# A two-layer attention block on one core: first scores between the query units, another order at the opening and the group norm, an earlier check of sums

## The chip, the cores and the metric

The kernel runs on one core of one Trainium2 chip. The metric is device time in microseconds (us) of one launch, measured over several executions. Names of engines as in the profile: PE is TensorE's matmul, PEld its weight load, DVE VectorE, ACT ScalarE, POOL GpSimd, SP SyncE.

## The reference

Input x has the shape (8, 512, 32, 32) in float32: 8 batches, 512 channels, 1024 tokens. There are two layers in a row:

```python
# layer 0: layer norm over channels, 8 heads of 64, residual
xn = layer_norm(x_flat, gamma, beta)
q = xn @ Wq.T + bq; k = xn @ Wk.T + bk; v = xn @ Wv.T + bv
attn = softmax(q k^T / 8)          # per head
out = (attn v) @ Wo.T + bo + residual
# layer 1: group norm (32 groups), one head of 512, residual
h = group_norm(x, gamma, beta)
q = wq h + bq; k = wk h + bk; v = wv h + bv
attn = softmax(q^T k / sqrt(512))
return x + wp (attn v) + bp
```

## The kernel before

All products of 512 x 512 blocks and larger are done as seven half-size products instead of eight (a class `Product` with seven steps; each step is four matmul records of 128x512 or eight of 128x256). The sums of blocks that this needs are made once per weight by GpSimd, and per batch by VectorE (the differences T1 to T4 of an activation, `T_h` in the profile for the layer norm's result). In an opening, two weight products are formed: a = wk^T wq for layer 1's scores, and m = wp wv. Names that recur: lns and lnq are VectorE's sums of x and of its centred squares, over which PE forms mean and var for the layer norm; psbm, psbo and psu are groups of 32 one-column matmuls that make three small vectors; pm and pv are PE's sums of the group norm's statistics mv and gdev; "half clock" is a granted clock of 0.5 for PE's array. PE's order is fixed by hand; the order of the other engines is the scheduler's.

```python
def sums_of_blocks(engine, w, view=lambda t: t):      # GpSimd, for the weights
    engine.tensor_add(w["S1"], w["21"], w["22"])
    engine.tensor_sub(w["S2"], w["S1"], w["11"])
    engine.tensor_sub(w["S3"], w["11"], w["21"])
    engine.tensor_sub(w["S4"], w["12"], w["S2"])
...
def add_operands(b, names):                            # VectorE, T1 to T4
    for n in names:
        ...
        nc.vector.tensor_sub(wide(b[n]), wide(b[l]), wide(b[r]))
...
nq = natural(wq, "q1")                 # 32 transposes on PE, 2 copies on ACT
ln = LayerNorm(0, x_next)
for k in range(NH):
    ln.sums(k)                         # lns, on VectorE
ln.mean()                              # 2 x 2 matmul records
for k in range(NH):
    ln.centre(k); ln.squares(k)        # lnq, on VectorE
nk = natural(wk, "k1")
columns(bm, ...)                       # psbm: 32 one-column matmul records
product(wa, nq, nk, "a", 0)
ln.deviation()                         # var
...
product(wa, nq, nk, "a", 1)
... sums_of_blocks(nc.gpsimd, wo), and of w_v, w_q, wa, wm on GpSimd too ...
nv = natural(wv, "v1")
columns(bo, ...)                       # psbo
product(wm, nv, wp, "m", 0); product(wm, nv, wp, "m", 1)
kt = all_of(project("k0", wk_now, bias_of("bk0"), hb))
columns(ua, ...)                       # psu: 32 one-column matmul records
vts = all_of(project_v("v0", wv_now, hb))
qt = all_of(project("q0", wq_now, bias_of("bq0"), hb))
```

## Time and profile before

| | before |
|---|---|
| median of 3 executions when the prediction was made | 3069.1 us (3067.01 to 3069.84) |
| span of the profiled execution | 3066.4 us |
| PE busy | 3008.8 us, 98% |
| first key projection starts | 73.37 us |
| first value projection starts | 101.11 us |
| a batch from its query projection to the next key projection | 148.4 us |
| last matmul to end of span | 8.69 us |

PE is the bound: there are 57.6 us in which it does not work. A change of order can win only parts of this, what stands in the opening at a low clock, and matmuls that it takes away. How the lines of the page, the waits, the chain and the opening are read is told in the prediction. Here are lines in PE's timeline (start, duration, instructions; in brackets the idle time and who ended it). The group norm's boundary of the second batch:

```profile
685.50 1.88 PE L330 MATMUL x_k<-x,w_k 128*128 128x512 f32 x4
687.88 0.39 PE L489 MATMUL pm<-mv,grp 128*128 128x4 f32 x2 [0.51 <-DVE mv L485]
```

The last batch's output projection:

```profile
2880.01 2.46 PE L330 MATMUL x_out<-o,w_o 128*128 128x512 f32 x4 [2.64 <-DVE u(0, 0)_out L599]
2882.26 3.15 PE L330 MATMUL z_out<-o,w_o 128*128 128x512 f32 x4
2885.25 1.88 PE L330 MATMUL x_out<-T_o,w_o 128*128 128x512 f32 x4
```

Here the reader is to see the 2.64 us wait, and behind it 2.46 and 3.15 us for groups that take 1.88 elsewhere: a stretch at half clock.

### The profile page before, as it was taken

The numbers are of one execution on the slowest core, as the hardware profiler recorded it, in microseconds if no ns is written. First come the engines' busy times: TensorE is split into PE (matmuls) and PEld (weight loads), VectorE is DVE, ScalarE is ACT, GpSimd is POOL, SyncE is SP. The second block draws the span as 40 slices with busy tenths as digits, with TensorE's granted clock in tenths as the row PEclk, the third lists the DMA queues.
The fourth block names the chain that finished last, engine by engine and source line by source line (L and its number), as shares of the span: only waits on it lengthen the run. The fifth ranks groups of instructions, "written<-read, shape, count | busy, mean of one in ns | idle before, by whom it ended". The sixth has DMA issues, their size and how long they took to land.

```text
span 3066.4 us, 26320 instructions
## 1 busy us (share of the span) xinstructions
PE 3008.8 (98%) x10098; PEld 1391.7 (45%) x10098; DVE 1807.9 (59%) x2442; ACT 1016.2 (33%) x1319; POOL 48.5 (2%) x57
## 2 busy tenths in 40 slices
PE   7999999999999999999999999999999999999898
PEld 4533455334553345433564345533455334553344
DVE  4288453874448744586446855378553785537744
ACT  3264212623136230362204612155121642215230
POOL 5000000000000000000000000000000000000000
PEclk8999999999999999999999999999999999999999
DMA  7201322012220213203032030310412004220101
GB/s 261 106 15 35 120 86 97 1 56 99 96 87 1 96 59 106 76 4 127 24 107 76 4 127 29 129 49 8 147 55 103 25 11 144 72 79 11 49 4 53
DMA packets 70616, 217.04 MB, mean 71 GB/s; under 512 B 12817, under 2 KB 16913, under 8 KB 64337
## 3 DMA queue, kind: packets, MB, share of 16 engines
q1 hardware_dynamic: 62032, 204.23, 18.9%
q0 software_dynamic: 2112, 11.01, 0.9%
q8 instruction: 81, 1.33, 0.2%
q10 hardware_dynamic: 6336, 0.03, 0.1%
q14 instruction: 55, 0.44, 0.0%
HBM read 156.00 MB, written 59.24 MB: 70 GB/s over the span
## 4 chain that ended last, share of the span: by engine, by line
PE 88%; DVE 7%; ACT 3%; issue 1%; DMA 1%; ACTq 0%; SPq 0%; DVEq 0%
PE acc L562 13%; PE s L546 13%; PE x_s L347 5%; PE x_o L355 5%; PE y_s L347 4%; PE y_o L355 4%; PE z_s L347 4%; PE z_o L355 4%; PE x_qa L330 3%; PE x_vm L339 3%; PE x_v L339 3%; PE x_q L330 3%; PE x_k L330 2%; PE y_qa L330 2%; PE y_q L330 2%; PE x_out L330 2%
## 5 line engine op out<-in xcount | busy, mean ns | idle before, releaser
L549 ACT ACTIVATE p<-s 128x1024 f32<-128x1024 f32 x512 | 483.7, 1032 | 202.3 <-PE s L546 201.7
L555 DVE TENSOR_TENSOR sum<-sum,p 128x1024 f32<-128x1024 f32 x384 | 470.0, 1224 | 53.3 <-ACT p L549 19.9
L562 PE MATMUL acc<-p,v 128*64 128x512 f32 x2048 | 465.9, 598 | 0.0
L546 PE MATMUL s<-q,k_again 64*128 64x512 f32 x1792 | 416.2, 603 | 10.0 <-ACT p L549 10.0
L546 PEld LDWEIGHTS s<-q,k_again 64*128 64x128 f32 x1792 | 163.1, 186 | 260.9 <-issue 188.3
L562 PEld LDWEIGHTS acc<-p,v 128*64 128x64 f32 x2048 | 136.2, 136 | 315.0 <-issue 296.0
L638 ACT ACTIVATE p<-p 128x512 f32<-128x512 f32 x128 | 80.6, 630 | 141.1 <-DVE p L278 141.1
L347 PE MATMUL x_s<-S_qa,T_gn 128*128 128x512 f32 x256 | 120.9, 594 | 0.0
L355 PE MATMUL x_o<-T_p,S_vm 128*128 128x512 f32 x256 | 115.1, 592 | 0.0
L553 DVE TENSOR_TENSOR sum<-p,p 128x1024 f32<-128x1024 f32 x64 | 78.2, 1222 | 58.2 <-ACT p L549 58.2
L278 DVE TENSOR_TENSOR p<-u(1, 1)_s,y_s 128x512 f32<-128x512 f32 x32 | 22.0, 687 | 123.9 <-ACT u(1, 1)_s L360 123.9
L565 ACT COPY o<-acc 128x512 f32<-128x512 f32 x64 | 37.6, 587 | 154.8 <-PE acc L562 154.8
L278 DVE TENSOR_TENSOR y<-u(1, 1)_o,y_o 128x512 f32<-128x512 f32 x16 | 11.0, 688 | 130.8 <-ACT u(1, 1)_o L360 130.8
L377 ACT ACTIVATE u(0, 0)_k<-x_k,vecs 128x512 f32<-128x512 f32 x16 | 11.0, 687 | 224.4 <-PE x_k L330 224.4
L347 PEld LDWEIGHTS x_s<-S_qa,T_gn 128*128 128x128 f32 x256 | 48.0, 190 | 63.0 <-issue 61.1
L355 PEld LDWEIGHTS x_o<-T_p,S_vm 128*128 128x128 f32 x256 | 48.6, 190 | 61.2 <-issue 61.2
L330 PE MATMUL x_out<-T_o,w_o 128*128 128x512 f32 x128 | 60.9, 598 | 2.9 <-DVE u(0, 1)_out L599 2.9
L546 PE MATMUL s<-q,k 64*128 64x512 f32 x256 | 59.5, 603 | 1.7 <-ACT p L549 1.7
L330 PE MATMUL x_qa<-T_gn,w_a 128*128 128x512 f32 x128 | 60.8, 597 | 0.0
L339 PE MATMUL x_vm<-w_m,T_gn 128*128 128x256 f32 x256 | 60.5, 379 | 0.0
L347 PE MATMUL y_s<-S_qa,gn 128*128 128x512 f32 x128 | 60.2, 592 | 0.0
L347 PE MATMUL z_s<-qa,T_gn 128*128 128x512 f32 x128 | 60.2, 592 | 0.0
(328 smaller groups left out, 4457.2 us busy)
## 6 DMA issues: line engine op xcount, KB each, us to landing
x<-in_x_dram SPq DMA_DIRECT2D x32, 512.0 KB, 9.3
xr<-in_x_dram SPq DMA_DIRECT2D x64, 256.0 KB, 3.8
x_away<-x SPq DMA_DIRECT2D x32, 512.0 KB, 3.0
x1r<-x_away SPq DMA_DIRECT2D x64, 256.0 KB, 3.8
out_dram<-y SPq DMA_DIRECT2D x64, 256.0 KB, 2.2
w_o<-saved_o SPq DMA_DIRECT2D x8, 1792.0 KB, 7.0
w_a<-saved_a SPq DMA_DIRECT2D x8, 1792.0 KB, 7.3
w_m<-saved_m SPq DMA_DIRECT2D x8, 1792.0 KB, 8.4
```

Of the source, the lines that this page charges most:

```text
L278: nc.vector.tensor_add(self.dest(i, k), u, ps)
L330: nc.tensor.matmul(dst, a[:, k, ts(r, P)], b[:, k, :], start=(opens and k == 0), stop=(k == 1), skip_group_check=True)
L339: nc.tensor.matmul(dst[:, ts(m, CB)], b[:, k, ts(2 * r + m, P)], a[:, k, :], start=(opens and m == 0 and k == 0), stop=(k == 1), skip_grou ...
L347: nc.tensor.matmul(dst, b[:, k, ts(r, P)], a[:, k, :], start=(opens and k == 0), stop=(k == 1), skip_group_check=True)
L355: nc.tensor.matmul(dst, a[:, m, ts(r, P)], b[m // 2][:, m % 2, :], start=(opens and m == 0), stop=(m == NM // 2 - 1), skip_group_check=True)
L546: nc.tensor.matmul(s[:, ts(i, HB)], self.k[m // 4][r, ts(m % 4, P)], self.q[r, :], start=True, stop=True)
L549: nc.scalar.activation(p, s, AF.Exp, scale=1.0 / float(D) ** 0.5)
L553: nc.vector.tensor_add(self.sum, self.p[0], p)
L555: nc.vector.tensor_add(self.sum, self.sum, p)
L562: nc.tensor.matmul(self.acc[i * D : (i + 1) * D, :], value_of(self.vt, m, self.c * P + i * D, D), self.p[m][:, ts(i, HB)], start=(m == 0), ...
L565: nc.scalar.copy(self.o, self.acc)
L638: nc.scalar.activation(dest(i, k), dest(i, k), AF.Exp, scale=float(C) ** -0.5)
```

## The change

Its intent: PE gets work while x and the vectors arrive, loses 32 small matmuls, starts attention's exponentials earlier, and meets fewer waits at the group norm, at the last output projection and at the end. Cut to its core:

```diff
-    wq = load_chunks("q1")
+    wq, wk = (load_chunks(n) for n in ("q1", "k1"))
+    bq1_row = half_tile("bq1_row")
+    nc.sync.dma_start(out=bq1_row, in_=...)
     x_next = load_x(0)
-    wk, wv, wp = (load_chunks(n) for n in ("k1", "v1", "p1"))
+    wv, wp = (load_chunks(n) for n in ("v1", "p1"))
 ...
         nq = natural(wq, "q1")
+        nk = natural(wk, "k1")
         ln = LayerNorm(0, x_next)
         ... sums ...
+        product(wa, nq, nk, "a", 0)
         ln.mean()
         ... centre, squares ...
-        nk = natural(wk, "k1")
+        nv = natural(wv, "v1")
+        product(wa, nq, nk, "a", 1)
         columns(bm, ...)
-        product(wa, nq, nk, "a", 0)
         ln.deviation()
         ...
-        product(wa, nq, nk, "a", 1)
-        nv = natural(wv, "v1")
-        columns(bo, ...)
         product(wm, nv, wp, "m", 0)
+        columns(bo, ...)
         product(wm, nv, wp, "m", 1)
+        for c in range(NC):
+            nc.vector.scalar_tensor_tensor(t, wk[c], 1.0, bq1_row, ..., accum_out=ua[:, c : c + 1])
         kt = all_of(project("k0", ...))
-        columns(ua, ...)
 ...
+            first = Pair(b, 0, 0, qt, kt, vts, ot)
+            first.scores(range(3))
+            q_units[1].rest()
 ...
-            groups[0][0].scores(groups[0][1])
+            first.scores(range(3, NM // 2))
 ...
-                    k_units[1].step((1, 2, 3, 1)[n])
+                    k_units[1].step((2, 1, 3, 1)[n])
 ...
-            a_units[0].step(1)
+            a_units[0].step(2)
             meanwhile(3)
-            a_units[0].step(1)
 ...
-                           banks_of(f"out_{b}", r, shared), after)
+                           banks_of(f"out_{b}", r, shared, own="x"), after)
 ...
+            if not more:
+                all_checks()
             o_units, value_sums = whole.values(vm)
```

The two query units also get PSUM tiles of their own (`apart`), and the check that stood behind the last batch became the function `all_checks`.

More of the change, by code (lines that the diff above doesn't have):

```diff
@@ L142, in load_chunks @@
         return chunks
-    wq = load_chunks("q1")
+    wq, wk = (load_chunks(n) for n in ("q1", "k1"))
+    bq1_row = half_tile("bq1_row")
+    nc.sync.dma_start(out=bq1_row, in_=vecs["bq1"].rearrange("(a c) -> a c", a=1).to_broadcast((P, C)))
     x_next = load_x(0)
-    wk, wv, wp = (load_chunks(n) for n in ("k1", "v1", "p1"))
+    wv, wp = (load_chunks(n) for n in ("v1", "p1"))
     ident = const.tile([P, P], F32, tag="ident", name="ident")
@@ L259, in columns @@
                 nc.tensor.matmul(ps[:, o : o + 1], lhs(c, o), rhs(c), start=(c == 0), stop=(c == NC - 1))
-        if plus is None:
-            nc.vector.tensor_copy(dst, ps[:, :NC])
-        else:
-            nc.vector.tensor_add(dst, ps[:, :NC], vt[:, VECS.index(plus), :])
+        nc.vector.tensor_add(dst, ps[:, :NC], vt[:, VECS.index(plus), :])
     class Product:
@@ L312, in rest, with banks_of @@
             self.step(len(STEPS) - self.done)
-    def banks_of(tag, r, shared):
+    def banks_of(tag, r, shared, own=""):
         def banks(to):
@@ L318, in banks @@
                 return bank(f"y_{tag}_{r}")
-            if shared is None:
+            if shared is None or to in own:
                 return wide_psum(f"{to}_{tag}_{r}")[:, :HB]
@@ L709, in values, with all_checks @@
             return [unit(r) for r in range(2)], lambda: sums_of_blocks(nc.vector, w, wide)
+    def all_checks():
+        one = small.tile([P, 1], F32, tag="one", name="one")
+        nc.vector.tensor_reduce(one, checks[:, : n_checks[0]], mybir.AxisListType.X, ALU.add)
+        ps = bank("ps_check")
+        nc.tensor.matmul(ps[:, :1], ones, one, start=True, stop=True)
+        ok = small.tile([P, 1], F32, tag="ok", name="ok")
+        nc.vector.tensor_scalar(ok, ps[:, :1], SUM_LIMIT, None, ALU.is_le)
+        nc.vector.tensor_scalar(flag, ok[:1, :], -1.0, 1.0, ALU.mult, ALU.add)
     def bias_of(n):
@@ L724, in fast_path @@
             ln.sums(k)
+        wa = big_slots("a")
+        product(wa, nq, nk, "a", 0)
         ln.mean()
@@ L728, in fast_path @@
             ln.squares(k)
-        nk = natural(wk, "k1")
+        nv = natural(wv, "v1")
+        product(wa, nq, nk, "a", 1)
         columns(bm, lambda c, oc: wp[c][:, ts(oc, P)], lambda c: vec("bv1", c), "bm", "bp1")
-        wa = big_slots("a")
-        product(wa, nq, nk, "a", 0)
         ln.deviation()
@@ L736, in fast_path @@
         hb = operands(ln.result())
+        add_operands(hb, ("T1", "T2", "T3", "T4"))
         wk_now = w_first["k"](nc.gpsimd)
-        add_operands(hb, ("T1", "T2", "T3", "T4"))
-        product(wa, nq, nk, "a", 1)
         wv_now = w_first["v"](nc.gpsimd)
@@ L742, in fast_path @@
         save_w("o", wo)
-        nv = natural(wv, "v1")
+        wm = big_slots("m")
+        product(wm, nv, wp, "m", 0)
         columns(bo, lambda c, oc: wo[f"{oc // 2 + 1}{c // 2 + 1}"][:, c % 2, ts(oc % 2, P)],
                 lambda c: vec("bv0", c), "bo", "bo0")
-        wm = big_slots("m")
-        product(wm, nv, wp, "m", 0)
         product(wm, nv, wp, "m", 1)
@@ L753, in fast_path @@
         save_w("m", wm)
+        for c in range(NC):
+            t = half_tile(f"uat_{c}")
+            nc.vector.scalar_tensor_tensor(t, wk[c], 1.0, bq1_row, ALU.mult, ALU.mult, accum_out=ua[:, c : c + 1])
         kt = all_of(project("k0", wk_now, bias_of("bk0"), hb))
-        columns(ua, lambda oc, c: nk[oc][:, ts(c, P)], lambda oc: vec("bq1", oc), "u", None)
         vts = all_of(project_v("v0", wv_now, hb))
-        qt = all_of(project("q0", wq_now, bias_of("bq0"), hb))
+        q_units, qt = project("q0", wq_now, bias_of("bq0"), hb, True)
+        q_units[0].rest()
         for b in range(B):
@@ L761, in fast_path @@
             ot = {"tag": f"o_{b}"}
-            pairs = [Pair(b, hf, c, qt, kt, vts, ot) for hf in range(NH) for c in range(NC)]
+            first = Pair(b, 0, 0, qt, kt, vts, ot)
+            first.scores(range(3))
+            q_units[1].rest()
+            pairs = [first] + [Pair(b, hf, c, qt, kt, vts, ot) for hf in range(NH) for c in range(NC) if hf + c > 0]
             groups = [(p, range(g * NM // 2, (g + 1) * NM // 2)) for p in pairs for g in range(2)]
             x_next = load_x(b + 1) if more else None
-            groups[0][0].scores(groups[0][1])
+            first.scores(range(3, NM // 2))
             for i, (p, ms) in enumerate(groups):
@@ L856, in fast_path @@
                 vts = all_of(project_v(f"v{b + 1}", wv_next, hb))
-                qt = all_of(project(f"q{b + 1}", wq_next, bias_of("bq0"), hb))
-        one = small.tile([P, 1], F32, tag="one", name="one")
-        nc.vector.tensor_reduce(one, checks[:, : n_checks[0]], mybir.AxisListType.X, ALU.add)
-        ps = bank("ps_check")
-        nc.tensor.matmul(ps[:, :1], ones, one, start=True, stop=True)
-        ok = small.tile([P, 1], F32, tag="ok", name="ok")
-        nc.vector.tensor_scalar(ok, ps[:, :1], SUM_LIMIT, None, ALU.is_le)
-        nc.vector.tensor_scalar(flag, ok[:1, :], -1.0, 1.0, ALU.mult, ALU.add)
+                q_units, qt = project(f"q{b + 1}", wq_next, bias_of("bq0"), hb, True)
+                q_units[0].rest()
 @with_exitstack
```

## The prediction

> **What bounds the kernel now.** I read the page first, then the list of waits of TensorE (PE), then the chain that ended last and the timeline at the four places that the change touches. The page says that PE is the bound and hardly ever stops:
>
> ```profile
> PE 3008.8 (98%) x10098; PEld 1391.7 (45%) x10098; DVE 1807.9 (59%) x2442; ACT 1016.2 (33%) x1319; POOL 48.5 (2%) x57
> ```
>
> So all that can be won without less matmul work is 3066.4 - 3008.8 = 57.6 us, plus stretches at a low clock. The list of PE's waits tells where the idle time is (columns: total, times, longest):
>
> ```profile
> PE s L546 <- ACT p L549: 11.7, 14, 1.3
> PE mean L430 <- DVE lns L438: 7.8, 2, 4.4
> PE pst_q L238 <- DMA w_q<-in_L_conv_wq_dram: 5.8, 2, 5.1
> PE pm L489 <- DVE mv L485: 5.8, 8, 2.2
> PE y_k L330 <- DVE k L278: 5.5, 7, 0.8
> PE psw_m L249 <- ACT nat_v L241: 2.9, 1, 2.9
> PE x_out L330 <- DVE u(0, 1)_out L599: 2.9, 7, 0.4
> PE x_out L330 <- DVE u(0, 0)_out L599: 2.6, 1, 2.6
> ```
>
> Three of these belong to the opening (mean, pst_q, psw_m), pm to the group norm, the last one to the eighth batch. The first line is a trap: it looks like the scores at the start of a batch, but in the timeline its 14 cases are 1.30 and 0.37 us (7 times each), beside the LayerNorm's var in the middle of a batch, where ScalarE loads two tables. At the start of a batch the chain shows PE working without a break (columns: start, us, what; it continues with the next batch's groups alike):
>
> ```profile
> 147.96 1.77 PE y_q L330 x4
> 149.72 7.07 PE s L546 x32
> 156.79 3.58 PE acc L562 x16
> 160.38 3.63 PE s L546 x16
> ```
>
> The opening, on PE alone (timeline: start, us, then the group, idle time before it in brackets):
>
> ```profile
> 14.07 2.07 PE L430 MATMUL mean<-lns,ones_c 128*128 128x512 f32 x2 [4.36 <-DVE lns L438]
> 19.59 2.08 PE L430 MATMUL mean<-lns,ones_c 128*128 128x512 f32 x2 [3.45 <-DVE lns L438]
> ...
> 29.74 9.56 PE L249 MATMUL psw_a<-nat_k,nat_q 128*128 128x512 f32 x16
> ...
> 40.85 7.03 PE L249 MATMUL psw_a<-nat_k,nat_q 128*128 128x512 f32 x16
> ...
> 57.15 16.38 PE L249 MATMUL psw_m<-w_p,nat_v 128*128 128x512 f32 x32 [2.93 <-ACT nat_v L241]
> ```
>
> The same 16 matmuls take 9.56 us the first time and 7.03 the second; the stretch table gives a mean granted clock of 0.66 for 25 to 35 us and 0.53 for 51 to 62 us, and 1.00 between and after. The key projection starts at 73.37 us.
>
> **What the Trainium skill says.** "TensorE: Matmul & The Clock Gate", section "What's actually happening": the array runs at half clock by default, and after an idle window of some 3.4 us, and at full clock after a busy one; the window runs freely. The trace agrees: half clock follows the one-column matmuls (psbm, psbo) and the idle stretches, and ends some 5 us into the dense work after them. The same page, "LDWEIGHTS (loading the stationary operand)", says that a weight load costs by its columns, P / 1.2 ns, so a one-column matmul costs a full load of 128: 107 ns. The trace: the 32 matmuls of psu take 3.47 us of the chain, 0.108 each. "ScalarE: Activation LUTs", section "What ACT_TABLE_LOAD costs": about 1283 ns a load; the trace has 1.28. "Runtime: NRT & Kernel Launch", section "Instruction fetch mechanics": a taken branch out of the fetched pages waits for its target. The trace ends with such a branch on the flag: last vector work done at 3059.8, span over at 3066.4.
>
> **Part 1, the opening.** The order of instructions becomes: transposes of w_q and w_k, product a (half 0), mean, transposes of w_v, a (half 1), psbm, var, m (half 0), psbo, m (half 1), key projection. w_k is loaded before x, so PE has work while x comes. When can a start? In the trace ScalarE copies the first transposes at 12.55 (it issues the vectors' DMAs until 11.2 and then loads a table for 1.28), two copies in 1.93 us; w_k takes x's place in the queue and lands at about 12. So the four copies end at about 16.4, and a can start at about 15.5. From there I add full-clock durations: a 6.9, mean 1.7, transposes 1.9, a 6.9, psbm 4.75, var 1.7, m 6.9, psbo 4.75, m 6.9: 42.4 us, so 57.9. To this come losses by the half clock. Before, psbm with a cost 0.9 + 2.6, psbo with m 1.0 + 2.5. After, both column groups still cut dense work; depending on where the window falls I take 2.7 each, and 2.3 for a's cold start: 7.7. One more wait: VectorE's order puts bm (which needs psbm) ahead of the last LayerNorm sum, so var's second half waits some 0.4 us. Key projection at 57.9 + 7.7 + 0.4 = 66.0 instead of 73.4: **-7.4 us**. Does the LayerNorm hold it up? x lands some 3.5 us later (1.25 MB more ahead of it, less what the weights' place behind it gives), but mean comes after a anyway (about 25); var ends at about 43 instead of 40.9, which moves the last differences T_h from 64.2 to some 66, and the key projection needs the second of them only 3.4 us after its start.
>
> The 32 matmuls psu go: **-3.5 us**. In their place VectorE does four 128x512 products with a sum (0.75 us each by the like instruction of L703, 3 us), before x is there, while it is idle.
>
> **Part 2, first scores between the two query units.** No matmul is added, and by the chain above no wait is removed: each of the 8 groups of scores is fed in time. What is added is two changes between full-array and 64-row matmuls. A change has a price in the chain: two groups of 16 take 2 x 3.63 = 7.26, one of 32 takes 7.07, so 0.19 us per group. Two more per batch, 8 batches: 16 x 0.19 = **+3.0 us**. The units get PSUM tiles of their own; with three wide tiles, unit 1 needs the tile of score 0, whose exponential should be ready 0.5 us before PE asks. I see no new wait.
>
> **Part 3, group norm.** Two steps of the key projection (3.4 us) instead of one before pm: mv is late by 0.51 us in the seven batches with a next one, and that goes: 7 x 0.51 = **-3.6 us**. Then one step (1.7 us) instead of two must cover mean to gdev, 0.75 us of four small VectorE instructions, which now follow one 0.69 us addition: it just fits. gn is needed one step earlier by the second step of qa, but pv comes 0.7 us earlier too. The last batch (2.2 + 0.8 + 2.1 us of waits) has no such filling and stays.
>
> **Part 4, own x tile in the output projection.** The 2.6 us wait of the last batch goes in part: z is still shared and written behind the next VectorE addition, and VectorE's chain sets the pace soon after. I take **-1.2 us**. The seven waits of 0.42 us are on the unit's own tile and stay.
>
> **Part 5, the check ahead of the values.** ps_check costs 0.28 us wherever it stands; at the end the engines can reach their branch earlier, except SyncE, which still issues the last output. **-0.4 us**.
>
> Sum: -7.4 - 3.5 + 3.0 - 3.6 - 1.2 - 0.4 = -13.1, so 3069.1 - 13.1 = 3056.0 us.
>
> **Rivals.** (a) The LayerNorm becomes the opening's bound: x later, so T_h late, and PE waits on DVE in k or in var. For it: VectorE is busy 15.2 of 17.2 us from 40 on. Against it: the margins above. It would take some 4 us: 3060. (b) The first scores do help, because ScalarE starts its exponentials earlier, and the switch is free: for it, 8 exponentials at 0.93 us apart just keep up with 7.07 us of scores; against it, no wait is in the list. 3053. (c) The group norm's wait only moves, from pm to pv or to qa: 3059.6. (d) Half clock after each column group lasts two windows more often than I take, or never happens: 3 us either way.
>
> **Range and chances.** The parts are independent, each uncertain by 1 to 3 us, the opening most; three runs of before spread over 2.8 us. That gives 3049 to 3062. Two per cent is 61 us, more than all of PE's idle time: faster by over 2% 0.01, within 2% 0.98, slower 0.01.
>
> **What would show it.** Right: the key projection's first matmul at 63 to 69 us; no psu; PE's list without mean, psw_m and the seven pm waits of 0.5; the s group at a batch's start split in two, with no gap, and a batch there 0.4 us longer; the y_k and middle-of-batch s waits as before. Wrong: a wait of k or var on DVE of over 2 us, a new wait at pv, qa or at x_q for ACT p, or batches longer than before.

## The result

The changed kernel took 3054.86 us (median of 6 executions, 3053.93 to 3056.45), the kernel before 3069.47 (6 executions, 3067.01 to 3070.32). The ratio is 0.9954, 95% interval 0.9941 to 0.9967. Ratios here are the mean time of one kernel's runs over that of the other's of the same rounds, so not quite the ratio of the medians that are quoted. It is a gain of 14.6 us, below 2%. Predicted were 3056.0 us. The page says:

```profile
PE 3002.2 (98%) x10066; PEld 1385.8 (45%) x10066; DVE 1820.0 (60%) x2449; ACT 1017.1 (33%) x1319; POOL 50.0 (2%) x57
```

PE has 32 matmul records less (psu) and works 6.6 us less. The waits of PE (total, times, longest):

```profile
PE s L545 <- ACT p L548: 11.7, 14, 1.3
PE pst_q L240 <- DMA w_q<-in_L_conv_wq_dram: 5.7, 2, 4.9
PE y_k L329 <- DVE k L277: 5.5, 7, 0.8
PE var L429 <- DVE lnq L437: 4.1, 1, 4.1
PE x_out L329 <- DVE u(0, 1)_out L598: 4.0, 8, 1.1
PE z_k L329 <- DVE k L277: 2.3, 1, 2.3
PE pm L488 <- DVE mv L484: 2.2, 1, 2.2
...
PE z_out L329 <- DVE x L277: 1.7, 1, 1.7
```

The waits of mean, of psw_m, the seven short ones of pm and x_out's on u(0, 0) are gone. New are var on lnq 4.1, z_k on k 2.3, z_out on x 1.7 and, among the lines left out, two in front of w_k's transposes (1.3 on its transfer, 0.9 on ScalarE's copies); x_out's list has an eighth case of 1.1. The trace, cut at the starts of the stages, says where the time went:

| stretch | before | after | difference | predicted |
|---|---|---|---|---|
| start to first value projection (opening, and psu) | 101.11 | 92.82 | -8.3 | -10.9 |
| query projection to the next key projection, 8 batches (the last, to the end of attention: 143.4 and 143.8) | 148.4 each | 148.8 each | +3.2 | +3.0 |
| output projection to layer 1's scores, 7 batches | 62.7 each | 61.8 each | -6.4 | -3.6 |
| the same in the last batch | 61.22 | 60.03 | -1.2 | -1.2 |
| layer 1's value projection to the end, last batch | 83.28 | 81.93 | -1.35 | -0.4 |
| span | 3066.4 | 3052.3 | -14.1 | -13.1 |

The sum was hit, and two of its terms were not. The opening in PE's timeline:

```profile
15.65 8.62 PE L251 MATMUL psw_a<-nat_k,nat_q 128*128 128x512 f32 x16
...
27.58 7.03 PE L251 MATMUL psw_a<-nat_k,nat_q 128*128 128x512 f32 x16
34.45 3.63 PE L261 MATMUL psbm<-vecs,w_p 128*128 128x1 f32 x32
...
43.14 2.08 PE L429 MATMUL var<-lnq,ones_c 128*128 128x512 f32 x2 [4.10 <-DVE lnq L437]
...
55.86 8.81 PE L251 MATMUL psw_m<-w_p,nat_v 128*128 128x512 f32 x16
64.51 1.88 PE L329 MATMUL x_k<-x,w_k_first 128*128 128x512 f32 x4
...
75.52 2.64 PE L329 MATMUL z_k<-T_h,w_k_first 128*128 128x512 f32 x4 [2.27 <-DVE k L277]
```

The key projection starts at 64.51, earlier than the 66.0 predicted, in spite of a wait of 4.10 that had been put at 0.4. Then it takes 28.3 us instead of the 24.3 of before (27.74 less 3.47 for psu): it waits 2.27 and runs on at half clock. What VectorE and GpSimd did in these places (their timelines, put together in order of time):

```profile
38.83 1.27 POOL L192 TENSOR_TENSOR w_v_first<-w_v,w_v_first 128x512 f32<-128x512 f32 x1
38.92 4.17 DVE L437 TENSOR_TENSOR lnq<-lnq 128x512 f32<-128x512 f32 x1
40.05 1.26 POOL L194 TENSOR_TENSOR w_v_first<-w_v_first,w_v 128x512 f32<-128x512 f32 x1
41.27 1.25 POOL L193 TENSOR_TENSOR w_v_first<-w_v_first 128x512 f32<-128x512 f32 x1
...
64.22 5.37 DVE L409 TENSOR_TENSOR T_h<-x,x 128x1024 f32<-128x1024 f32 x1
```

The last addition of lnq, 128x512, takes 4.17 us. The same kind of instruction (lns at 20.03) takes 0.69 with GpSimd idle. It starts 0.09 us after the first of three GpSimd sums in a row and ends at 43.09, 0.6 us after the third: it looks as if it stood still until GpSimd paused. The four T_h differences take 2.89, 4.64, 5.37 and 5.36 beside other sums; undisturbed ones of this size take 1.22 (before: 1.21, 1.22, 4.94, 2.94). The second of them was there at 64.29, ahead of its use at 67.94. The step of z_k that waits needs the fourth, there at 74.87, and an empty tile z, which VectorE's addition k, queued behind the fourth, empties at 75.47; the step starts at 75.52.

The Trainium skill has this: "SBUF — State Buffer", section "SBUF: two separate sides", says that VectorE and GpSimd share a pair of ports as an exclusive lock, that a VectorE instruction with two SBUF inputs takes part in it against a GpSimd instruction that reads SBUF, and that the loser is blocked for the whole of the winner's instruction. The trace agrees in kind, but here VectorE was held for three GpSimd sums and not for one (4.17 us against 1.27). Up to here this is a reading of one trace.

The batch start in the chain (start, us, what):

```profile
127.46 1.83 PE y_q L329 x4
129.29 2.78 PE s L545 x12
132.07 1.91 PE x_q L329 x4
133.98 1.72 PE z_q L329 x4
...
144.33 4.49 PE s L545 x20
```

No wait is there, as before; the first group after the scores takes 1.91 instead of 1.72. The skill's "TensorEngine Tiling (Array Packing)", section "Key Properties", says that a change of tiling mode drains TensorE; scores are 64-row matmuls, projections 128-row ones, and a change between them costs 0.19 us here. That the drain is all of it, no run shows. Group norm:

```profile
677.51 1.88 PE L329 MATMUL x_k<-x,w_k 128*128 128x512 f32 x4
679.23 1.88 PE L329 MATMUL z_k<-x,w_k 128*128 128x512 f32 x4
680.95 0.28 PE L488 MATMUL pm<-mv,grp 128*128 128x4 f32 x2
```

Everything follows at 1.72 us a group, and pm has no wait.

### The profile page after: what moved, and what is told of

The parts are those of the page before. It is cut to its first block, busy times and chain, and to the rows that moved or that the text cites. A ratio compares the mean times of both kernels' runs of the same rounds, so it can differ in the third digit from the quotient of the medians.

```text
span 3052.3 us, 26260 instructions
## 1 busy us (share of the span) xinstructions
PE 3002.2 (98%) x10066; PEld 1385.8 (45%) x10066; DVE 1820.0 (60%) x2449; ACT 1017.1 (33%) x1319; POOL 50.0 (2%) x57
## 3 DMA queue, kind: packets, MB, share of 16 engines
q8 instruction: 81, 1.33, 0.2%
## 4 chain that ended last, share of the span: by engine, by line
PE 89%; DVE 6%; ACT 3%; issue 1%; DMA 1%; ACTq 0%; SPq 0%; DVEq 0%
PE acc L561 13%; PE s L545 13%; PE x_s L346 5%; PE x_o L354 5%; PE y_s L346 4%; PE y_o L354 4%; PE z_o L354 4%; PE z_s L346 4%; PE x_qa L329 3%; PE x_vm L338 3%; PE x_q L329 3%; PE x_v L338 3%; PE x_k L329 2%; PE y_qa L329 2%; PE y_q L329 2%; PE y_vm L338 2%
```

## The experiments

Eleven runs were made, all with correct results: the first four below (kernel before: 3068.57 us, 11 executions), the next four (3067.6, 9 executions), the last three (3067.67, 9 executions).

### The first scores in one group again (e1_scores_last)

```diff
-            first.scores(range(3))
             q_units[1].rest()
+            first.scores(range(3))
```

> The changed kernel with the first three scores moved behind the second query unit, so one group of scores again as before; everything else as changed. Theory: part 2 removes no wait and pays two more changes between full-array and 64-row matmuls per batch. The trace of the changed kernel has the stretch from the query projection to the next projection longer by 0.39 us in each of 8 batches, 3.1 us in all. So this kernel should be 3.1 us faster than the changed one, about 3051.7 us, ratio to the kernel before 0.9942 where the changed one has 0.9954, and the stretch back at 148.4. Rival: the early scores give ScalarE its start, so the scores after the query units would now wait for exponentials: a wait of s on ACT p at each batch's start, and 3055 us or more. Second rival: the 0.39 us come from the units' own PSUM tiles, not from the split: then the stretch stays at 148.8 and the time at 3054.9.

Measured: 3052.75 us (6 executions, 3042.2 to 3055.57), ratio 0.9945 [0.9933, 0.9958]. The stretch is 148.45 us in the first batch and 148.38 in the others, as before the change, and no wait of s at a batch's start appears. The tiles of their own stayed, so the split alone costs the 0.4 us. The chain shows the one group:

```profile
141.02 7.07 PE s L545 x32
```

7.07 here against 2.78 + 4.49 = 7.27 for the two groups, and 0.19 more in x_q. In time the gain is less plain than in the trace, as the executions lie 5 us apart; one took 3042.2, which is taken up below.

### The first scores in three groups (e2_scores_twice)

```diff
-            first.scores(range(3))
+            first.scores(range(2))
+            q_units[1].step(3)
+            first.scores(range(2, 3))
             q_units[1].rest()
```

> The changed kernel with the first scores in one place more: two scores, three steps of the second query unit, one score, the other four steps, then the last score. That is one more break of the query unit per batch, with two more changes of matmul shape. If such a pair of changes costs 0.39 us, the batch stretch is 149.2 instead of 148.8 and the whole 8 x 0.39 = 3.1 us longer than the changed kernel: about 3058 us, ratio 0.9964. Rival (the cost belongs to the units' tiles, or was paid once for something else): the stretch stays at 148.8 and the time at 3054.9.

Measured: 3057.51 us (5 executions, 3056.2 to 3061.53), ratio 0.9971 [0.9958, 0.9984]; the stretch is 149.25 and 149.18 us. The dose is right: 148.4, 148.8, 149.2 for one, two and three groups.

```profile
129.33 1.92 PE s L545 x8
131.24 1.91 PE x_q L329 x4
...
136.59 1.06 PE s L545 x4
137.65 1.91 PE y_q L329 x4
```

Each group of scores and each group of the projection behind it holds the same 0.19 us: 4 score matmuls take 1.06, 8 take 1.92, so 0.215 each and 0.20 besides.

### The group norm's order alone (e3_gn_only)

```diff
-                    k_units[1].step((1, 2, 3, 1)[n])
+                    k_units[1].step((2, 1, 3, 1)[n])
 ...
-            a_units[0].step(1)
+            a_units[0].step(2)
             meanwhile(3)
 ...
-            a_units[0].step(1)
```

> The kernel before with the new order at the group norm only (two steps of the key projection ahead of pm, two of qa ahead of the last key step). The prediction gave it 7 x 0.51 = 3.6 us, the listed wait. The traces have the stretch from the output projection to qa 0.77 us shorter per batch and the next one 0.14, together 0.91 x 7 = 6.3 us, because a wait costs more than its listed gap: the gap counts from the modelled end of the matmul ahead, which lies 0.16 us behind the moment at which the next could start. Expected 3069.5 - 6.3 = 3063.2 us, ratio 0.9979. If the prediction's reading was right and the rest comes from other parts of the change: 3065.9, ratio 0.9988. Rival: the wait moves to pv or qa, and the time stays at 3069.5.

Measured: 3062.93 us (5 executions, 3061.32 to 3067.15), so 5.6 less than before by the medians; the ratio is 0.9988 [0.9975, 1.0], closer to the second figure than to the first, since two of the five executions were long; the interval holds both. The traces decide between the two: the stretch from the output projection to layer 1's scores is 6.0 us shorter over the seven batches (432.7 against 438.7 in sum), not 3.6. In all nine traces with the new order this sum is 431.6 to 432.9, in the four without it 438.4 to 438.7. The eighth batch, which the edit does not help, was 1.2 us longer in this execution (62.39 against 61.22). Both numbers of that batch hold half clock, and this varies between executions of one kernel.

### The check alone (e4_check_only)

```diff
+            if not more:
+                all_checks()
             o_units, value_sums = whole.values(vm)
 ...
-        one = small.tile([P, 1], F32, tag="one", name="one")
-        ... (the seven lines of the check behind the last batch)
```

> The kernel before with the check of sums ahead of the last values only. The prediction gave it 0.4 us. The traces have the stretch to the last values 0.15 us longer and from there to the end 1.50 shorter, net 1.35: PE's own branch on the flag, 4.33 us at the end of the kernel before, is over before the end. Expected 3068.1 us, ratio 0.9996, and the distance from PE's last matmul to the span's end about 7.2 us instead of 8.7. Rival: the end is set by SyncE, which issues the last output, and nothing is won: 3069.5 and 8.7. At this size the time alone will hardly tell; the trace's stretch must.

Measured: 3065.33 us (5 executions, 3063.34 to 3067.92), ratio 0.9992 [0.9979, 1.0005], which can't tell it from nothing. In the trace the stretch from layer 1's value projection to the end is 82.21 us against 83.28, so 1.1 us less: 0.15 more for the check's matmul in its new place, and 1.2 less behind it. PE's last matmul is 7.51 us ahead of the end instead of 8.69. The thirteen traces agree: the stretch is 83.04 to 83.28 us in the four with the check at the end and 81.84 to 82.26 in the nine with it moved. The ends of the two timelines, before and with this edit:

```profile
3058.96 0.13 DVE L866 TENSOR_SCALAR flag<-ok 1x1 int32<-1x1 f32 x1
3059.08 0.75 DVE L703 SCALAR_TENSOR_TENSOR y<-y,bm,x1r 128x512 f32<-128x512 f32 x1
3059.86 0.34 SPq L704 DMA_DIRECT2D out_dram<-y  x1
```

```profile
3058.44 0.75 DVE L703 SCALAR_TENSOR_TENSOR y<-y,bm,x1r 128x512 f32<-128x512 f32 x1
3059.22 0.34 SPq L704 DMA_DIRECT2D out_dram<-y  x1
```

From the issue of the last output to the end of the span it is 3066.40 - 3059.86 = 6.54 us before and 3064.46 - 3059.22 = 5.24 here. VectorE's last three instructions on the output need 2.2 us in both, so its small instructions for the check, in between, cost nothing: what is won lies behind the last output. There, in the kernel before, all engines but SyncE load the flag at 3059.1, as soon as it is written, and PE's branch on it takes 4.33 us, to 3064.07. With the check moved the flag is known some 50 us ahead of the last output, and PE is through before the end. The branch in both traces (the source view counts it to PEld's sequencer; min, median and max in ns, then the start):

```profile
L1210 PEldq COMPARE_BRANCH  x1: 4335/4335/4335, 3059.7 to 3059.7; - x1
```

```profile
L1215 PEldq COMPARE_BRANCH  x1: 3775/3775/3775, 3052.1 to 3052.1; - x1
```

The rival, that nothing is won, falls by the traces.

### The opening alone (e5_opening_only)

The kernel before with only the hunks of the opening (loads, order, `ua` by four VectorE products).

> The kernel before with part 1 only: the new order of the opening and the four VectorE products in place of psu. The trace of the changed kernel starts the first value projection at 92.8 us instead of 101.1, so 8.3 us less; the prediction had 10.9. Expected 3069.5 - 8.3 = 3061.2 us, ratio 0.9973, with the waits of var on lnq (4.1 us) and z_k on k (2.3 us) there as in the changed kernel. If those waits come from another part of the change, they are absent here and the gain is 12 us or more.

Measured: 3061.85 us (5 executions, 3060.39 to 3065.63), ratio 0.9983 [0.997, 0.9997]. The first value projection starts at 92.81 us. The waits are there: var 3.9, z_k 2.5. So they belong to the opening's new order. The span is 7.7 us shorter instead of 8.3, as the first batch took 1.25 us longer, with a wait of s on ACT of 0.7 that no other trace has: ScalarE's table load for the exponentials started at 142.48, 3.3 us after the end of its work before. Why it came late stays open.

### GpSimd's sums held behind T4 (e6_hold_all)

```diff
-    def sums_of_blocks(engine, w, view=lambda t: t):
+    def sums_of_blocks(engine, w, view=lambda t: t, behind=None):
         w = {n: view(t) for n, t in w.items()}
+        if behind is not None:
+            for n in ("S1", "S3"):
+                engine.tensor_copy(w[n][:, 0, 0:1], behind[:, 0, 0:1])
 ...
-        wv_now = w_first["v"](nc.gpsimd)
+        wv_now = w_first["v"](nc.gpsimd, hb["T4"])
         ... the same for w_q, w_o, w_a and w_m
```

> The changed kernel with GpSimd's block sums of w_v, w_q, w_o, w_a and w_m made to wait for the last difference T_h (tiny copies out of T4 ahead of them); only w_k's stay early. Theory: VectorE's additions of two SBUF operands are drawn out while GpSimd does the same kind of work: the last lnq addition takes 4.17 us beside w_v's sums and 0.69 alone, the T_h differences 2.9 to 5.4 beside others and 1.22 alone. Without GpSimd beside them: last lnq addition 0.7, T_h 1.2 each, var's wait 4.1 down to about 0.6, no wait of z_k, no half clock behind it. That is 3.5 + 2.3 + about 1.7 = 7.5 us: key projection at about 61, first value projection at about 85.3, time about 3047.4, ratio 0.9929. Rival: the long durations come from something else (transfers, ScalarE, matmuls reading the same memory): durations and time stay as in the changed kernel, 3054.9. Second rival: the held sums end too late for the value projection and a wait of v on w_v takes the place.

Measured: 3046.87 us (5 executions, 3045.86 to 3047.76), ratio 0.9932 [0.9919, 0.9946]. The key projection starts at 61.06, the first value projection at 85.25. VectorE's timeline:

```profile
38.96 0.69 DVE L440 TENSOR_TENSOR lnq<-lnq 128x512 f32<-128x512 f32 x1
...
54.36 1.23 DVE L412 TENSOR_TENSOR T_h<-x,x 128x1024 f32<-128x1024 f32 x1
55.69 1.22 DVE L412 TENSOR_TENSOR T_h<-x,T_h 128x1024 f32<-128x1024 f32 x1
```

and the one wait that is left of the two:

```profile
PE var L432 <- DVE lnq L440: 0.6, 1, 0.6
```

The lnq addition is back from 4.17 to 0.69 us though it starts at the same 38.9, and T_h takes 1.22. Everything else that ran there still runs: in the same trace GpSimd issues transfers of the weights from 38.85 to 42.6, and PE works. So it is GpSimd's sums that held VectorE up, and not its transfers. The held sums were in time for the value projection. The first rival falls, and so does the second.

### Only the sums of w_o, w_a, w_m held (e7_hold_oam)

The same edit without w_v and w_q.

> As the run that holds all, but only the sums of w_o, w_a and w_m wait for T4; those of w_v and w_q stay early. Theory: w_v's sums still lie beside lnq, so var's wait of 4.1 us stays and the key projection starts at 64.5; the T_h differences, which have only w_o, w_a and w_m beside them, take 1.2 us each, so z_k's wait of 2.3 us and the half clock behind it (about 1.7 us) go: first value projection at about 88.8, time about 3050.9, ratio 0.9940. Rival: no change in durations, 3054.9.

Measured: 3050.83 us (5 executions, 3049.95 to 3051.82), ratio 0.9945 [0.9932, 0.9959]. var waits 4.1 us as in the changed kernel, z_k has no wait, the key projection takes 24.2 us, the first value projection starts at 89.35. The two collisions are separate: w_v's sums with lnq cost some 4 us (e7 against e6), those of w_o, w_a and w_m with T_h some 4 us (e7 against the changed kernel).

### The own x tile alone (e8_ownx_only)

```diff
-            if shared is None:
+            if shared is None or to in own:
 ...
-                           banks_of(f"out_{b}", r, shared), after)
+                           banks_of(f"out_{b}", r, shared, own="x"), after)
```

> The kernel before with the own PSUM tile for x in the output projection only. By the traces 1.33 us in the last batch and nothing in the others (prediction 1.2): 3068.1 us, ratio 0.9996. Rival: the seven waits of x_out on u(0, 1) of 0.42 us go too, then 7 x 0.58 = 4.1 us more: 3064.0. The time alone will hardly tell; the stretch from the output projection to qa in the last batch must be 34.0 instead of 35.3.

Measured: 3066.58 us (5 executions, 3065.09 to 3067.34), ratio 0.9995 [0.9982, 1.0009]. The stretch from the output projection to qa in the last batch is 34.02 us, which looks like the 34.0 expected. But it proves nothing: the same stretch is 34.14 us in e4 and 33.78 in e5, which don't have this part. PE's waits there, with the own tile (this run), then without it (e4):

```profile
2880.11 1.98 PE L330 MATMUL z_out<-o,w_o 128*128 128x512 f32 x4 [1.72 <-DVE x L278]
...
2886.62 1.98 PE L330 MATMUL x_out<-T_o,w_o 128*128 128x512 f32 x4 [1.09 <-DVE u(0, 1)_out L599]
```

```profile
2879.59 1.98 PE L330 MATMUL x_out<-o,w_o 128*128 128x512 f32 x4 [2.63 <-DVE u(0, 0)_out L599]
...
2886.89 1.98 PE L330 MATMUL x_out<-T_o,w_o 128*128 128x512 f32 x4 [0.17 <-DVE u(0, 1)_out L599]
```

1.72 + 1.09 = 2.81 with it, 2.63 + 0.17 = 2.80 without: the wait was divided and not removed. The 1.33 us that the two first traces showed go with the half clock behind the wait in the one execution of before, told above. Of the four traces without the own tile two have this half clock (before and e3), of the nine with it none. So shorter waits may spare it, and the part may be worth half a microsecond on average; four traces are too few to say so.

### The changed kernel once more (after_again)

No edit; it stood beside the next two.

> The changed kernel unaltered, so that it stands beside the next two on the same chip. Expected: 3054.9 us, ratio 0.9954, with the var wait of 4.1 us and the z_k wait of 2.3 in its trace.

Measured: 3053.54 us median of 5, ratio 0.9954 [0.9941, 0.9968]. Four executions took 3052.9 to 3054.15 us and one 3045.59, and the profile happened to be of this one. The expected waits of var and z_k are not in it. Its span is 3043.9, its first value projection starts at 83.53 instead of 92.82. The same program, the same addition, and the first GpSimd sum of w_v:

```profile
37.01 1.28 DVE L437 TENSOR_TENSOR lnq<-lnq 128x512 f32<-128x512 f32 x1
...
38.77 1.28 POOL L192 TENSOR_TENSOR w_v_first<-w_v,w_v_first 128x512 f32<-128x512 f32 x1
```

In this execution mean ran 1.2 us earlier (product a took 7.70 us instead of 8.62, its half clock ending sooner), so lnq's last addition came at 37.0 and was through at 38.3, before the sums of w_v began at 38.8. There the two engines just miss each other; in the usual execution they meet, and the difference is some 8 us (3053.6 for the other four in the mean). The T_h differences are drawn out here too (2.21, 2.10, 2.96, 4.85), but the last ends at 65.3, before z_k asks for it at 67.9. It fits the same cause, by one execution. The 3042.2 us execution of e1, 8 us or more below its other five, may be of this kind, but has no trace.

### Both gains together (e9_best)

The edits of e6 and e1 together.

> The changed kernel with GpSimd's sums held behind T4 (all but w_k's) and the first scores in one group behind both query units: the two experiments that helped, together. If their gains are of different places they add: 3046.9 (held sums alone) - 3.1 (scores) = 3043.8 us, ratio 0.9922, batch stretch 148.4 and first value projection at 85.3. Rival: with the held sums the early scores had become useful in the first batch (GpSimd's sums now lie later and slow VectorE's sums of exponentials): then the first batch's stretch is longer than 148.5 and the time stays near 3046.9.

Measured: 3042.73 us (5 executions, 3042.44 to 3045.08), ratio 0.9922 [0.9908, 0.9935]. The first value projection starts at 84.44, the first batch's stretch is 148.46. The gains add.

### One-column matmuls between the dense ones (e10_spread)

```diff
     def product(dst, lhs, rhs, n, g, beside=None, each=2, between=None):
         ...
                 nc.tensor.matmul(ps[:, ts(k, C)], lhs[oc][...], rhs[oc], ...)
+                for _ in range(each if beside is not None else 0):
+                    next(beside, None)          # one column of psbm or psbo
+            if k == 0 and between is not None:
+                next(beside, None)
+                between()                       # var
 ...
-        columns(bm, ...)
-        ln.deviation()
+        product(wm, nv, wp, "m", 0, columns(bm, ...), 4, ln.deviation)
 ...
-        product(wm, nv, wp, "m", 0)
-        columns(bo, ...)
-        product(wm, nv, wp, "m", 1)
+        product(wm, nv, wp, "m", 1, columns(bo, ...))
```

> As the run with both, and the one-column matmuls of psbm and psbo no longer in groups of 32: psbm's lie between the matmuls of the first half of m (half 0), psbo's between those of m (half 1), two or four columns after each dense matmul, and var between the two halves of m (half 0). The same number of matmuls. Theory (the prediction's): the half clock after each column group comes from the group's own low use of the array. In the run with held sums 6.83 us of half clock lie at 39.1 to 45.9, some 3.4 us lost, and var still waits 0.6. Spread, no window is idle: key projection at about 57 instead of 61, time about 3040, ratio 0.991. Rival: the share of dense work while they are mixed (about 0.43 of every 0.63 to 0.86 us) is too small and the half clock comes all the same, now over more of the dense work: key projection at 61 or later, 3044 or more.

Measured: 3038.76 us (4 executions, 3038.58 to 3041.98), ratio 0.9909 [0.9894, 0.9924]. The key projection starts at 56.16. The windows view from 50 to 55 us (seventh column PEclk, the granted clock), first of e9, then of this run:

```profile
50.00:55.00 5.00, 5.00 (x21) 2.94 (x21) 3.13 (x4) 2.55 (x5) 0.00 (x0) 0.68 0.00 0
```

```profile
50.00:55.00 5.00, 5.00 (x25) 3.18 (x24) 3.75 (x4) 2.98 (x5) 0.00 (x0) 1.00 0.00 0
```

PE counts as busy for all 5 us in both, yet the clock is 0.68 in the one and 1.00 in the other. From 17 us on this run has no half clock until the last batch. But a group of 32 does not always bring it: in none of the four traces that have psu does half clock follow it, and of the eight traces with the new opening's grouped psbo, three (e1, e5, e6) show none behind it. What decides this no run shows, and e10 has one trace. This is the best version here: 28.9 us below the kernel before by the medians, 14.8 below the changed kernel.

## Why the prediction was right or wrong

The total was right to 1.1 us, inside the range. Of its five parts one had the right size (2), two had the right mechanism and were too small (3 and 5), one was too large and wrong in a step (1), and one was wrong (4). The errors cancelled, so the hit of the total is in part luck. The signs that the prediction named for right came true (the key projection's start, the waits gone, the split scores without a gap), and one for wrong too: waits of var and k on DVE of over 2 us.

**Part 1, the opening (predicted -10.9, measured -8.3).** The start of product a (15.65 for 15.5) and the loss of psu were right. Two terms were mis-sized. "psbm 4.75 ... psbo 4.75" were too long: each took 3.63, because 4.75 was psbo's time before, at 49.5 to 54.2 and so in part at half clock, and the half clock was then added again. "7.7" for half clock was too much: up to the key projection, a's cold start cost 1.6, var and m (half 0) 1.5, m (half 1) 1.8, together 4.9. The reading behind it, that half clock follows the one-column groups and the idle stretches, left out that in the same trace psu leaves none and that the clock is 1.00 from 15 to 25 us, after and between two idle stretches; rival (d), that it comes more or less often than taken, stays open. Against this stands the step that failed: "var's second half waits some 0.4 us" was 4.1, and "the key projection needs the second of them only 3.4 us after its start", with the last T_h at 66, became 74.9 and a wait of 2.27 with half clock behind it. The second difference was in time; the fourth, and the addition queued behind it, were not. What was missing in that step is not the order on any one engine but two engines beside each other: the LayerNorm's additions were taken at the durations of the old trace, while in the new order other sums of GpSimd lay on top of them (e5, e6, e7, after_again). The before trace had held the sign: two of its four T_h differences took 4.94 and 2.94 us instead of 1.22. Rival (a) is what happened in kind, and more of it (4.1 + 2.3 us of waits on VectorE against its some 4), though not for its reason, a late x: mean follows product a without a wait. The over-long column groups hid it in the sum.

**Part 2, first scores (+3.0, measured +3.2).** Right, by its mechanism: no wait removed, two more changes of shape per batch at 0.19 us. e1 and e2 show it from both sides, and rival (b) falls.

**Part 3, group norm (-3.6, measured -6.4, alone -6.0).** The mechanism was right: the wait went and moved nowhere, so rival (c) falls. The size was off. "mv is late by 0.51 us ... 7 x 0.51" took the listed gap for the cost. A gap ends a pipeline of matmuls that start every 0.43 us and last 0.59 each by the model, so it costs 0.16 more than listed; pm itself is 0.1 us shorter without the wait, and 0.14 us goes at the reordered qa step.

**Part 4, own x tile (-1.2, in the first two traces -1.2, alone 0.0).** Wrong, though the traces seemed to agree. "The 2.6 us wait of the last batch goes in part" failed: 2.80 us of waits became 2.81 (e8 against e4). VectorE's chain sets the pace at once, not "soon after".

**Part 5, the check (-0.4, measured -1.35, alone -1.1).** The mechanism was right, the term too small: "the engines can reach their branch earlier" is worth 1.2 to 1.5 us behind the last output, less 0.15 for the matmul that still costs its place. The prediction let SyncE, which issues the last output, set nearly all of the end, and the 4.33 us of PE's branch was longer than that. Why 5.2 us are still left behind the last output, no run here tests; in e4's trace VectorE's branch comes at 3059.1 and its next instruction only at 3062.2.

With the parts as measured alone (-8.3, +3.2, -6.0, 0, -1.1) the sum is -12.2; the remaining 1.9 us of the span's 14.1 are put down to half clock in the one execution of before (1.2, last batch) and to the spread between executions.

## What to carry to other kernels

When a change moves one engine's work in time, look at what another engine will then be doing in the same microseconds: VectorE additions of two SBUF tensors should not lie beside GpSimd work of that kind on a critical path, and holding back GpSimd work that nobody needs yet won some 7 us here, by the spans of the traces, with a few one-column copies. Never take a difference between two single traces for the gain of a part before looking at the waits themselves and at the clock in that stretch; the part alone, on the same chip, tells it. Small matmuls in a group can leave the array at half clock behind them; in the one run that put them between dense matmuls they didn't.

## What the Trainium skill lacked or had wrong

- "SBUF — State Buffer", section "SBUF: two separate sides", has the lock, and that the loser waits for the winner's whole instruction. It lacks that VectorE can lose several times in a row: a 0.69 us addition took 4.17 us beside three GpSimd sums of 1.26 us that followed each other, and 0.69 when they were held back.
- "TensorEngine Tiling (Array Packing)", section "Key Properties", says that a change of mode drains TensorE, but has no price. The runs show 0.19 to 0.20 us per change, some 0.4 us for one more interruption, linear over one, two and three groups.
- "TensorE: Matmul & The Clock Gate", section "What's actually happening", gives the half clock to idle windows, and does not say what counts as busy. A group of 32 one-column matmuls, in which the profile counts PE as busy all the time, brought it too in e9 (granted clock 0.68 from 50 to 55 us), and the same matmuls between dense ones did not in e10 (1.00); other groups of 32, psu's above all, brought none.
- "Perfetto Trace Analysis", which treats how PE's end times are reported, does not say by how much a listed gap of PE understates a wait: 0.51 us listed cost 0.66, since the gap is counted from the modelled end of a matmul that lasts 0.59 while the next could start after 0.43.
